# A convolution by butterfly matrices, attention and experts on one core: when input images are loaded in the first phase, and when GpSimd makes the butterfly matrices

## The chip, the cores and the metric

The kernel runs on one core of a Trainium2 chip. Its engines each work through their own queue in order: TensorE (PE, with its weight loads listed apart as PEld), VectorE (DVE), ScalarE (ACT), GpSimd (POOL) and SyncE (SP), which here issues the DMA transfers. The metric is the time on the device in microseconds (us); less is better.

## The reference, cut to what matters

The input is 32 images of 128 channels and 64 x 64 pixels, in 32-bit floats. Layer 0 normalises each image over groups of four channels, multiplies rows and columns by butterfly matrices (six levels of complex 2 x 2 twiddles each), mixes channels for every frequency with the weights, which have been transformed in the same manner, transforms back, keeps the real part and adds the input. Layer 1 is attention over channels and a mixture of eight experts of which two are used.

```python
def butterfly_lastdim(x, tw, increasing_stride):
    ...
        for idx in range(log_n):
            log_stride = idx if cur else log_n - 1 - idx
            stride = 1 << log_stride
            t = tw[blk, idx].reshape(n // (2 * stride), stride, 2, 2)
            xr = x.reshape(b, n // (2 * stride), 2, stride)
            x = jnp.einsum('djik,bdkj->bdij', t, xr).reshape(b, n)
...
x_f = tensor_product(xc, _c(k11), _c(k12), False)
w_f = tensor_product(wc, _c(kd1), _c(kd2), False) * math.sqrt(H * W)
prod = jnp.einsum('bihw,oihw->bohw', x_f, w_f)
out = tensor_product(prod, _c(k21), _c(k22), True)
return jnp.real(out)
...
x = x + _L0_conv_ref(_gn(x), L0_conv_weight, L0_conv_kd1, L0_conv_kd2, L0_conv_k11, L0_conv_k12, L0_conv_k21, L0_conv_k22)
t = _to_tokens(x)
t = t + _L1_attn_ref(_ln_t(t), L1_attn_Wk, L1_attn_bk, L1_attn_Wv, L1_attn_bv)
t = t + _L1_ffn_ref(_ln_t(t), L1_ffn_router_w, L1_ffn_router_b, L1_ffn_expert_w, L1_ffn_expert_b)
```

## The kernel before, in words

There are three phases. The first (lines 158 to 538) normalises each image and carries it into frequencies; the second (541 to 702) mixes the channels, frequency by frequency; the third transforms back and does layer 1. The change is in the first alone.

In the first phase an image goes through these steps. Eight loads of 256 KB, x(b, 0) to x(b, 7) (`load`, line 303), fill one of three image buffers. DVE takes statistics of 512 columns at a time (`stats`, line 310, "bn" in the plan); `group_norm` gathers them: an aggregate ("ag") on DVE, two tiny matmuls "g1" and "g2" with small DVE steps "gm" and "gr" behind each, a power on GpSimd ("gp", line 345, tile grstd), and four scalings "nm" of 1024 columns, from image 4 on by DVE (line 358). Then PE turns the image over in four groups ("pz", line 369), whose results ACT copies to z (line 379). The first transform runs along w in eight pieces ("pv", line 392; ACT copies each to v, line 403), the second along h in eight pieces ("pf", line 414). Each pf piece is copied to f, six of eight by DVE and pieces 3 and 7 by ACT ("fo", line 424), and SP stores it in two transfers of 256 KB ("fs", line 432). All the products of PE share four PSUM buffers, "ps"; a pf copy that is late holds one of them. There are four buffers f.

Images overlap: in slot s PE works on pz of image s, pv of image s - 1 and pf of image s - 2, in quarters: one pz, two pv, two pf. The order on PE is the order in which the program adds the operations.

The order on the other engines is the planner's (`Plan`, line 25). Every operation is added with an engine, an assumed duration, a due time in slots of 27.5, what it comes after, and what buffers it takes and frees. The planner plays this through: an engine that falls free takes, of the operations that are ready, the one with the earliest due time; it never breaks one off. The order so found is written out as the program. The durations and due times are nothing more than means of ordering; on the chip an instruction starts when the one before it in its queue is done and its own semaphores are there. So an "after" that isn't a true dependence of data only moves an instruction in its queue.

`norm(b)` (line 443) adds the loads of image b, due from slot b - 2 on, after the turning-over of image b - 3, whose buffer they take; the program calls it ahead of the PE work of slot b - 2. It then adds four statistics operations of two pieces each, due at slot b - 1. `butterfly(m, ...)` (line 435) builds one of the three transform matrices from its twiddles: m = 1 on DVE at the start, m = 0 (for the weights) and m = 2 (for the transform back) on GpSimd, with an opening step ("unit") and six levels (lines 207 to 222). `select` (line 241) also runs on GpSimd. m = 0 is due from slot 3.2 and m = 2 from slot 7. What comes of m = 2 is used by `output_matrices` ("wo", DVE) and lets the load "wm" of the weights start on SP.

Of the kernel before, what the change touches and what calls it, by code (L numbers as in the profile page):

```python
# [90 lines left out]
def kernel(  # L91
# [15 lines left out]
    nc = tc.nc  # L107
    B = x.shape[0]
# [11 lines left out]
    pf = dram.tile([n, n, P * n], F32, name="pf")  # L120
# [37 lines left out]
    with ExitStack() as ph1:  # L158
# [9 lines left out]
        made, xs, zs, vs, tile_of = {}, {}, {}, {}, {}  # L168
        on_pe = []

        def add(key, engine, us, at, run, after=(), take=(), free=(), late=0.0):
            after = [made[k] for k in after if k in made]
            if engine == "PE":
                after += on_pe[-1:]
            made[key] = plan.add(engine, us, SLOT * at, run, after, take, free, late)
            if engine == "PE":
                on_pe.append(made[key])
# [5 lines left out]
        def twiddles(m):  # L183
            def run():
                t = tile_of["tw", m] = bp.tile([P, 6, 2, 2, 2, n // 2], F32, tag="tw", name=f"tw{m}")
                for ax in range(2):
                    nc.sync.dma_start(
                        t[ax * n : (ax + 1) * n].rearrange("p a i j c d -> p (a i j c d)"),
                        tw[m, ax].rearrange("a i j c d -> (a i j c d)").partition_broadcast(n),
                    )  # L190
            return run

        def unit(m, eng):
            def run():
                cur = tile_of["bf", m] = bp.tile([P, 2, n], F32, tag="bf", bufs=2, name=f"bf{m}_in")
                eng.tensor_tensor(cur[:, 0, :], ident[:, 0:n], ident[:, n : 2 * n], ALU.add)
                if m == 1:

                    eng.tensor_copy(
                        cur[lo, 0, :].rearrange("p (k r) -> p r k", r=2), ident[lo, 0:n].rearrange("p (r k) -> p r k", r=2)  # L200
                    )
                eng.memset(cur[:, 1, :], 0.0)
            return run
# [99 lines left out]
        def load(b, k):  # L303
            def run():
                if k == 0:
                    xs[b] = xp.tile([P, NPIX], F32, tag="x", name=f"x{b}")
                nc.sync.dma_start(xs[b][:, k * 512 : (k + 1) * 512], xv[b][:, k * 512 : (k + 1) * 512])
            return run

        def stats(b, k):  # L310
            def run():
                if k == 0:
                    tile_of["bs", b] = st.tile([P, 8, 6], F32, name=f"gbs{b}", tag="gbs", bufs=2)
                for j in range(2 * k, 2 * k + 2):
                    nc.vector.bn_stats(tile_of["bs", b][:, j, :], xs[b][:, j * 512 : (j + 1) * 512])
            return run

        def group_norm(b):
# [116 lines left out]
        def butterfly(m, engine, eng, at, us):  # L435

            before = {1: [], 0: [("b1", 5), "wi", ("nm", 4, 3)], 2: [("b0", 5), "wd"]}[m]
            add(("tw", m), "SP", 0.9, -3.0 if m == 1 else at - 0.3, twiddles(m), before, (), (), 4.0)
            add((f"b{m}", -1), engine, 2 * us / 7, at, unit(m, eng), before)
            for idx in range(6):  # L440
                add((f"b{m}", idx), engine, us, at + 0.01 * idx, level(m, idx, eng), [("tw", m), (f"b{m}", idx - 1)])

        def norm(b):

            at = b - 1
            for k in range(8):
                add(
                    ("x", b, k), "SP", 0.45, b - 2 + 0.1 * k, load(b, k), [("pz", b - 3, g) for g in range(4)],
                    ("x",) if k == 0 else (), (), 4.0,
                )  # L450
            for k in range(4):
                add(("bn", b, k), "DVE", 1.4, at + 0.02 * k, stats(b, k), [("x", b, 2 * k), ("x", b, 2 * k + 1), ("nm", b - 2, 3)])

        def norm_on_pe(b, step):
            if not 0 <= b < B:
                return
            at = b - 0.9
            if step == 0:
                gn = tile_of["gn", b] = group_norm(b)
                add(("ag", b), "DVE", 0.4, at, gn[0], [("bn", b, k) for k in range(4)])  # L460
                add(("g1", b), "PE", 0.3, at, gn[1], [("ag", b)], ("ps",))
                add(("gm", b), "DVE", 0.7, at, gn[2], [("g1", b)])
            else:
                gn = tile_of.pop(("gn", b))
                add(("g2", b), "PE", 0.3, at, gn[3], [("gm", b)])
                add(("gr", b), "DVE", 0.25, at, gn[4], [("g2", b)], (), ("ps",))
                add(("gp", b), "POOL", 0.6 if b >= 4 else 1.6, at, gn[5], [("gr", b)])
                for k in range(4):
                    add(("nm", b, k), *(("DVE", 0.85) if b >= 4 else ("ACT", 1.05)), at + 0.01 * k, gn[6][k], [("gp", b)])

        def piece(kind, b, g, at):
            if not 0 <= b < B:
                return
            if kind == "pz":
                add(
                    ("pz", b, g), "PE", 1.0, at, turn_over(b, g), [("nm", b, k) for k in range(4)],
                    ("ps",), ("x",) if g == 3 else (),
                )
                for r in range(2):
                    add(  # L480
                        ("zo", b, g, r), "ACT", 1.2, at, turned(b, g, r),
                        [("pz", b, g)] + [("pv", b - 2, k) for k in range(8)] + ([("zo", b, 0, 0)] if g or r else []),
                        (), ("ps",) if r else (),
                    )
            elif kind == "pv":
                add(
                    ("pv", b, g), "PE", 1.12, at, along_w(b, g),
                    [("zo", b, k, r) for k in range(4) for r in range(2)] + ["wi"], ("ps",),
                )
                add(  # L490
                    ("vo", b, g), "ACT", 1.02, at, w_out(b, g),
                    [("pv", b, g)] + [("pf", b - 2, k) for k in range(8)] + ([("vo", b, 0)] if g else []), (), ("ps",),
                )
            else:
                add(("pf", b, g), "PE", 1.95, at, along_h(b, g), [("vo", b, k) for k in range(8)], ("ps",))
                on_act = g % 4 == 3
                add(("fo", b, g), "ACT" if on_act else "DVE", 1.02 if on_act else 1.22, at, h_out(b, g), [("pf", b, g)], ("f",), ("ps",))
                add(("fs", b, g), "SP", 0.9, at, store(b, g), [("fo", b, g)], (), ("f",), 5.0)
# [5 lines left out]
        norm_on_pe(0, 0)  # L504
        norm_on_pe(0, 1)
        for s in range(B + 2):
            if s + 2 < B:
                norm(s + 2)
            for g in range(4):
                at = s + 0.25 * g  # L510
                if g == min(s, 3) - 1:
                    norm_on_pe(s + 1, 0)
                piece("pz", s, g, at)
                for k in range(2):
                    piece("pv", s - 1, 2 * g + k, at + 0.04 + 0.04 * k)
                if g == min(s, 3) - 1:
                    norm_on_pe(s + 1, 1)
                for k in range(2):
                    piece("pf", s - 2, 2 * g + k, at + 0.12 + 0.07 * k)
            if s == 0:  # L520
                norm_on_pe(1, 0)
                norm_on_pe(1, 1)
            if s == 3:
                butterfly(0, "POOL", nc.gpsimd, 3.2, 4.5)
                add("sel", "POOL", 2.5, 3.5, select, [("nm", 4, 3)])
            if s == 6:
                add("wr", "PE", 0.6, 6.0, weight_rows, [("b0", 5), "sel"], ("ps",))
                add("wd", "DVE", 0.8, 6.0, weight_matrices, ["wr"], (), ("ps",))
                butterfly(2, "POOL", nc.gpsimd, 7.0, 4.5)
                add("wo", "DVE", 1.2, 9.0, output_matrices, [("b2", 5)])  # L530
                add("wm", "SP", 0.5, 10.0, weight_taps, [("b2", 5)], (), (), 4.0)
            if 12 <= s < 16:
                k = s - 12
                add(("wr", k), "POOL", 5.0, s - 0.5, onto_rows(k), ["wm", ("pf", s - 3, 4)], ("f",))
                add(("wt", k), "PE", 1.1, s, rows_turned(k), [("wr", k)], ("ps",))
                add(("we", k), "DVE", 1.25, s, rows_out(k), [("wt", k)], (), ("ps", "f"))
# [4 lines left out]
    with ExitStack() as ph2:  # L541
# [11 lines left out]
        made, tile_of = {}, {}  # L553
# [118 lines left out]
        for w in range(n):  # L672
# [9 lines left out]
            for half in range(2):  # L682
                for t in range(4):
                    at = w + 0.5 * half + 0.125 * t
# [632 lines left out]
```

## The time and the profile before

| | us |
|---|---|
| time, median of 3 runs (lowest to highest) | 6383.51 (6376.77 to 6393.35) |
| the profiled execution's own time | 6385.87 |
| span of that execution, first to last instruction | 6384.2 |
| busy over the span: PE / PEld / DVE / ACT / POOL | 6125.7 / 4796.3 / 4201.4 / 3757.4 / 4201.5 |

The first weight load of the second phase stands in the trace at 978.81 us, so the first phase is some 15% of the time. Its stretches, busy time of each engine with the number of instructions in brackets, then the granted share of TensorE's clock, the mean busy share of the 16 DMA engines and GB/s:

```profile
core 0: us, PE busy (x) PEld busy (x) DVE busy (x) ACT busy (x) POOL busy (x), PEclk, DMA share, GB/s
0.00:60.37 60.37, 26.32 (x588) 24.40 (x588) 35.33 (x122) 38.40 (x50) 4.95 (x19) 0.83 0.47 156
...
913.07:978.80 65.73, 64.60 (x1443) 62.71 (x1441) 22.05 (x18) 31.71 (x39) 1.08 (x1) 1.00 0.67 231
```

The first row is the filling of the pipeline, the second its draining. What lies between is in the prediction.

What SP waits for between 60 and 913 us (us in total, times, longest):

```profile
SPq L432 <- DVE f L424: 155.9, 71, 6.5
SPq L307 <- PE pz L369: 144.6, 26, 6.3
SPq L432 <- DVE gmv L324: 115.2, 27, 10.2
```

A line of a timeline reads: start, duration, engine, line, operation, tile written <- tiles read, shapes, how many alike were merged, and in square brackets how long the engine stood idle before it and what ended that. "issue" means that the profile shows nothing that the engine waited for.

### The profile page before, as it was taken

Reading aid. Unit: us, or ns where it says so; the run is one execution under the profiler, and the core shown is the slowest. Engines: PE = TensorE matmul, PEld = TensorE weight load, DVE = VectorE, ACT = ScalarE, POOL = GpSimd, SP = SyncE. Lnnn points to the kernel's source line nnn. Section 1 sums busy time; section 2 is a strip of 40 time slices with the busy share of each in tenths; the row PEclk is TensorE's granted clock in tenths of the full one; section 3 lists DMA queues with packets and bytes.
Section 4 is the critical chain, followed back from the end, with each engine's and each line's share of the span. In section 5 each row is a group of like instructions: output and inputs, shape, how many; then the busy total and the mean of one; then the engine's idle time right before and its main releaser. Section 6 shows DMA issues by size and latency. Waiting matters only on the chain. (4 is left out here: it accounts for less than half of the span.)

```text
span 6384.2 us, 218347 instructions
## 1 busy us (share of the span) xinstructions
PE 6125.7 (96%) x94922; PEld 4796.3 (75%) x94922; DVE 4201.4 (66%) x7626; ACT 3757.4 (59%) x7089; POOL 4201.5 (66%) x3780
## 2 busy tenths in 40 slices
PE   7999999999999999969999999999999999999987
PEld 7899998999999999966666666666666666666653
DVE  5555544555555555527787877778787878787776
ACT  6666663444444444446666667666666666666752
POOL 2110005666666666606888888888888888888889
PEclk9999999999999999989999999999999999999999
DMA  5666656666666666553121222222222212121100
GB/s 200 214 208 226 218 207 173 158 161 159 159 156 158 157 159 158 135 140 93 62 95 62 94 64 90 69 86 74 80 79 67 93 62 96 60 95 64 67 19 25
DMA packets 556966, 756.55 MB, mean 119 GB/s; under 512 B 58467, under 2 KB 321893, under 8 KB 551909
## 3 DMA queue, kind: packets, MB, share of 16 engines
q1 hardware_dynamic: 554096, 741.38, 38.8%
q8 instruction: 745, 12.21, 0.8%
q14 instruction: 217, 1.77, 0.1%
q10 hardware_dynamic: 1908, 1.19, 0.1%
HBM read 406.80 MB, written 335.54 MB: 116 GB/s over the span
## 5 line engine op out<-in xcount | busy, mean ns | idle before, releaser
L1189 PE MATMUL pe<-ew_sb,xT 128*128 128x512 f32 x4096 | 1983.0, 601 | 53.6 <-DVE tm L1200 53.3
L1200 DVE TENSOR_TENSOR tm<-pe,oh 128x512 f32<-128x512 f32 x2048 | 1354.3, 684 | 562.3 <-PE pe L1189 418.0
L1211 POOL TENSOR_TENSOR tm<-tm 128x512 f32<-128x512 f32 x1024 | 1306.8, 1291 | 314.5 <-DVE tm L1200 262.0
L1189 PEld LDWEIGHTS pe<-ew_sb,xT 128*128 128x128 f32 x4096 | 690.5, 191 | 525.0 <-issue 328.7
L623 PE MATMUL m<-f,s 128*64 128x64 f32 x32768 | 1069.9, 224 | 5.9 <-POOL s L574 4.5
L623 PEld LDWEIGHTS m<-f,s 128*64 128x64 f32 x32768 | 999.4, 138 | 67.6 <-POOL s L574 4.8
L574 POOL COPY s<-l 128x512 f32<-128x512 f32 x512 | 547.9, 1103 | 735.0 <-issue 656.2
L612 ACT COPY f<-g 128x1024 f32<-128x1024 f32 x512 | 518.5, 1013 | 672.2 <-PE g L601 645.0
L612 DVE COPY f<-g 128x1024 f32<-128x1024 f32 x512 | 627.1, 1225 | 348.9 <-PE g L601 340.9
L1214 POOL TENSOR_TENSOR tk<-tk,tm 128x256 f32<-128x256 f32 x1024 | 759.1, 741 | 80.3
L828 ACT COPY u<-pu 64x512 f32<-64x512 f32 x1024 | 593.4, 579 | 310.5 <-PE pu L818 299.6
L601 PE MATMUL g<-c,wst 9*128 9x128 f32 x16384 | 727.1, 287 | 25.6 <-ACT f L612 3.5
L1212 POOL TENSOR_TENSOR tm<-tm 128x512 f32<-128x512 f32 x512 | 652.5, 1274 | 40.1
L601 PEld LDWEIGHTS g<-c,wst 9*128 9x128 f32 x16384 | 580.5, 187 | 109.6 <-DVE f L612 69.2
L818 PEld LDWEIGHTS pu<-qw,r 128*128 128x128 f32 x4096 | 504.8, 197 | 169.5 <-ACT u L828 91.6
L633 DVE COPY o<-m 64x1024 f32<-64x1024 f32 x256 | 314.0, 1227 | 470.0 <-ACT o L633 395.8
L818 PE MATMUL pu<-qw,r 128*128 128x128 f32 x4096 | 523.7, 283 | 63.0 <-ACT u L828 52.8
L345 POOL TENSOR_TENSOR grstd<-gms,mhalf 128x1 f32<-128x1 f32 x32 | 17.7, 553 | 789.2 <-DVE gms L341 760.1
L414 PE MATMUL pf<-ph,v 128*128 128x128 f32 x4096 | 497.2, 280 | 20.5 <-issue 13.5
L576 POOL TENSOR_SCALAR s<-l 128x512 f32<-128x512 f32 x256 | 503.3, 1966 | 0.0
L414 PEld LDWEIGHTS pf<-ph,v 128*128 128x128 f32 x4096 | 471.8, 193 | 32.1 <-issue 15.0
L1227 ACT COPY so<-po 128x512 f32<-128x512 f32 x256 | 150.8, 589 | 572.5 <-issue 413.1
(165 smaller groups left out, 8624.6 us busy)
## 6 DMA issues: line engine op xcount, KB each, us to landing
xf<-f SPq DMA_DIRECT2D x512, 256.0 KB, 3.8
l<-xf SPq DMA_DIRECT2D x1024, 128.0 KB, 3.3
pf<-o SPq DMA_DIRECT2D x1024, 128.0 KB, 2.4
r<-pf SPq DMA_DIRECT2D x512, 256.0 KB, 4.6
x<-in_x_dram SPq DMA_DIRECT2D x256, 256.0 KB, 5.5
y<-in_x_dram SPq DMA_DIRECT2D x32, 2048.0 KB, 8.5
out_dram<-so SPq DMA_DIRECT2D x256, 256.0 KB, 2.0
tw<-in_tw_dram SPq DMA_DIRECT2D x6, 384.0 KB, 6.9
```

The costliest lines, as they stand in the source:

```text
L414: nc.tensor.matmul(pl[:, j * P : (j + 1) * P], vs[b][:, 8 * g + j, :], ph.rearrange("h r m -> h (r m)"), start=True, stop=True,)
L574: nc.gpsimd.tensor_copy(dst, src)
L601: nc.tensor.matmul(pg[g // 2][:, g % 2, m * P : (m + 1) * P], wst[rows, 16 * half + 4 * t + m, :], c[rows].rearrange("r h k -> r (h k)"), ...
L612: copy(f.rearrange("i m (g o) -> i m g o", g=2), tile_of["g", w, half, t][k].rearrange("i g (o m) -> i m g o", o=4))
L623: nc.tensor.matmul(ps[hh * n : (hh + 1) * n, q, :], s[:, h].rearrange("i k b -> i (k b)")[:, B * r : B * r + n], f[:, h, r, :], start=(r = ...
L818: nc.tensor.matmul(ps[:, k, :], rs[b, e][:, k * P : (k + 1) * P], qw.rearrange("w r m -> w (r m)"), start=True, stop=True,)
L828: nc.scalar.copy(u[r * n : (r + 1) * n, :, oh * n + 8 * e : oh * n + 8 * e + 8], ps[oh * n : (oh + 1) * n, :, r * n : (r + 1) * n].rearran ...
L1189: nc.tensor.matmul(ps, tile_of["xT", b, i // 4][:, i % 4, :], ew_sb[:, es, :].rearrange("d e c -> d (e c)"), start=True, stop=True,)
L1200: nc.vector.tensor_tensor(tile_of["tm", b, i // 2][:, i % 2, es, :], tile_of.pop(("pe", b, i, half)).rearrange("p (e c) -> p e c", c=P), t ...
L1211: nc.gpsimd.tensor_tensor(tm[:, k, 0:4, :], tm[:, k, 0:4, :], tm[:, k, 4:8, :], ALU.add)
L1212: nc.gpsimd.tensor_tensor(tm[:, :, 0:2, :], tm[:, :, 0:2, :], tm[:, :, 2:4, :], ALU.add)
L1214: nc.gpsimd.tensor_tensor(t[:, lo : lo + 2, :], t[:, lo : lo + 2, :], tm[:, :, m, :], ALU.add)
```

## The change

Three things are changed in the way the first phase is added to the plan.

Loads: from image 4 on, each load x(b, k) is added on its own behind the pf piece k of image b - 4 (`piece_of_image`), in the same slot b - 2 as before, and comes after that piece and after load k - 1. Images 0 to 3 keep their loads together.

Statistics: eight operations of one piece each in place of four of two, in the order of their pieces. `norm` for an image is added after the PE work of its slot in place of ahead of it, except for image 2.

GpSimd: the due times of the butterfly steps there, and of `select`, are put so late (99 slots on) that every other operation that is ready goes first. The loads of their twiddles keep their due times.

```diff
-                for j in range(2 * k, 2 * k + 2):
-                    nc.vector.bn_stats(tile_of["bs", b][:, j, :], xs[b][:, j * 512 : (j + 1) * 512])
+                nc.vector.bn_stats(tile_of["bs", b][:, k, :], xs[b][:, k * 512 : (k + 1) * 512])
...
             add(("tw", m), "SP", 0.9, -3.0 if m == 1 else at - 0.3, twiddles(m), before, (), (), 4.0)
+            at += 99 if engine == "POOL" else 0
             add((f"b{m}", -1), engine, 2 * us / 7, at, unit(m, eng), before)
...
+        def piece_of_image(b, k):
+
+            add(
+                ("x", b, k), "SP", 0.45, b - 2 + 0.1 * k, load(b, k),
+                [("pz", b - 3, g) for g in range(4)] + [("x", b, k - 1), ("pf", b - 4, k)],
+                ("x",) if k == 0 else (), (), 4.0,
+            )
+
         def norm(b):
 
             at = b - 1
+            for k in range(8) if b < 4 else ():
+                piece_of_image(b, k)
             for k in range(8):
-                add(
-                    ("x", b, k), "SP", 0.45, b - 2 + 0.1 * k, load(b, k), [("pz", b - 3, g) for g in range(4)],
-                    ("x",) if k == 0 else (), (), 4.0,
-                )
-            for k in range(4):
-                add(("bn", b, k), "DVE", 1.4, at + 0.02 * k, stats(b, k), [("x", b, 2 * k), ("x", b, 2 * k + 1), ("nm", b - 2, 3)])
+                add(("bn", b, k), "DVE", 0.7, at + 0.01 * k, stats(b, k), [("x", b, k), ("nm", b - 2, 3), ("bn", b, k - 1)])
...
-                add(("ag", b), "DVE", 0.4, at, gn[0], [("bn", b, k) for k in range(4)])
+                add(("ag", b), "DVE", 0.4, at, gn[0], [("bn", b, k) for k in range(8)])
...
         for s in range(B + 2):
-            if s + 2 < B:
-                norm(s + 2)
+            if s == 0:
+                norm(2)
             for g in range(4):
...
                 for k in range(2):
                     piece("pf", s - 2, 2 * g + k, at + 0.12 + 0.07 * k)
+                    if 4 <= s + 2 < B:
+                        piece_of_image(s + 2, 2 * g + k)
+            if 3 <= s + 2 < B:
+                norm(s + 2)
...
-                add("sel", "POOL", 2.5, 3.5, select, [("nm", 4, 3)])
+                add("sel", "POOL", 2.5, 99, select, [("nm", 4, 3)])
```

The order of the instructions on PE is the same in both programs. On GpSimd, the power step of image 8 stands behind the third of the six levels of m = 2 in place of the sixth, and that of image 5 one level of m = 0 earlier. On SP, in the middle of the phase, the loads of an image stand in this order among the stores: 0 and 1 behind the stores of piece 7 of the image before, 2 behind piece 1, 3 behind piece 2, 4 and 5 behind piece 3, 6 behind piece 5, 7 behind piece 6. On DVE the statistics of an image's pieces 6 and 7 and its aggregate stand ahead of the copy of pf piece 0, pieces 0 and 1 of the next image behind the copy of piece 1, and piece 2 between "gm" and "gr"; pieces 3 to 5 stand behind the copy of piece 5.

## The prediction

> **What bounds the kernel now.** The change touches only the first phase, so I read that stage alone, in four steps. First the busy times by stretch. I set the boundaries at starts of the first transpose group of an image (line 369): image 2 starts at 60.37 us, image 31 at 913.07; 540.95 to 570.12 is image 18, 885.74 to 913.07 image 30. Four short stretches are added. The columns are length, then busy time (instructions) of PE, PEld, DVE, ACT and POOL, then the granted clock, the DMA share, GB/s.
> ```profile
> 60.37:913.07 852.70, 812.54 (x19645) 775.40 (x19640) 469.69 (x666) 556.48 (x765) 82.33 (x230) 0.99 0.63 216
> 540.95:570.12 29.17, 27.85 (x679) 26.48 (x677) 16.20 (x24) 18.99 (x26) 0.55 (x1) 1.00 0.64 218
> 885.74:913.07 27.33, 27.22 (x678) 26.20 (x677) 10.84 (x14) 18.89 (x26) 0.55 (x1) 1.00 0.43 157
> 153.80:157.20 3.40, 3.40 (x18) 3.40 (x18) 1.88 (x2) 0.00 (x0) 0.00 (x0) 0.51 0.19 69
> 222.10:225.50 3.40, 3.40 (x19) 3.40 (x18) 1.34 (x4) 0.66 (x1) 3.19 (x10) 0.50 0.45 163
> 242.60:249.40 6.80, 4.82 (x118) 4.52 (x121) 6.63 (x14) 2.78 (x5) 0.57 (x2) 0.50 0.72 281
> 515.70:519.10 3.40, 3.40 (x16) 3.40 (x17) 2.63 (x5) 0.00 (x0) 0.00 (x0) 0.50 0.75 285
> ```
> PE sets the pace (812.54 of 852.70 us); DVE, ACT and DMA have room. Yet the 29 images take 852.70 / 29 = 29.40 us each, while image 30, during which no input image is loaded any more, takes 27.33 us with the same PE work and no gap. The pool to win from is (29.40 - 27.33) x 29 = 60 us, less some 5 us of extra PE work for the weights: 55 us.
>
> Second, what PE's weight loads wait for in that stretch (total, times, longest), and what DVE waits for:
> ```profile
> DVE gbs L315 <- DMA x<-in_x_dram: 99.3, 85, 14.7
> ...
> PEld pv L392 <- issue: 21.4, 94, 1.0
> ...
> PEld pf L414 <- issue: 15.0, 10, 2.5
> ...
> PEld pv L392 <- DVE f L424: 10.4, 15, 1.6
> ...
> PEld pz L369 <- issue: 6.0, 2, 5.6
> ...
> PEld pf L414 <- DVE f L424: 3.7, 11, 0.4
> ```
> Third, the timeline of image 18, which shows the wait for DVE being made:
> ```profile
> 545.34 2.92 DVE L315 BATCH_NORM_STATS2 gbs<-x 128x6 f32<-128x512 f32 x4 [2.36 <-DMA x<-in_x_dram]
> ...
> 549.33 0.69 DVE L315 BATCH_NORM_STATS2 gbs<-x 128x6 f32<-128x512 f32 x1 [1.07 <-DMA x<-in_x_dram]
> 549.94 1.21 DVE L424 COPY f<-pf 128x1024 f32<-128x1024 f32 x1
> ...
> 551.20 1.02 PEld L392 LDWEIGHTS pv<-pw,z 64*64 64x64 f32 x64 [1.16 <-DVE f L424]
> ```
> The statistics of image 20 stand on DVE ahead of the copy of pf. They wait for loads that SP issued in one burst, so the copy starts late, a PSUM buffer comes free late, and PE stops. Fourth, the timeline around image 8, where the wait called "issue" is really GpSimd:
> ```profile
> 228.61 0.16 DVE L341 TENSOR_SCALAR gms<-gps 128x1 f32<-128x1 f32 x1 [2.98 <-PE gps L338]
> ...
> 242.62 0.55 POOL L345 TENSOR_TENSOR grstd<-gms,mhalf 128x1 f32<-128x1 f32 x1
> ...
> 243.67 2.98 DVE L358 TENSOR_SCALAR x<-x,gms,grstd 128x1024 f32<-128x1024 f32 x4
> 244.55 1.57 PEld L369 LDWEIGHTS pz<-ident,x 128*128 128x128 f32 x8 [5.56 <-issue]
> ```
> The operand of grstd is there at 228.8, but grstd stands behind all six butterfly levels of the output twiddles, and PE idles 5.56 us for image 8.
>
> [...] the half-clock stretches above (0.50) are 3.4 us or twice that, and each lies at or behind one of PE's longest gaps (2.48 us before 153.64, 2.40 before 221.28, 5.56 before 244.55, 2.02 before 515.67). So a long gap costs more than itself. [...] The trace has that queue (q8, 745 packets, 12.21 MB), and I read the gaps inside PE groups that wait for nothing visible ("issue") as late refills: all those over 0.5 us, the 5.56 apart, lie 3 to 15 us into an image, which is where the loads and stores are densest. [...] From 538 to 551 us the DMA rows show nearly every slice at 9 tenths and 300 to 420 GB/s; from 561 to 565 they are idle.
>
> **The change part by part**, against the profiled execution's 6385.87 us (span 6384.2).
>
> 1. *GpSimd.* The operations are the same; the butterflies lose their due times, so grstd of image 8 comes after level three of six, and for image 5 one level earlier. A level takes 3.83 us (2.27 + 0.73 + 2 x 0.32 and hops). Level three ended at 231.2, so the normalisation (2.98 us) ends near 235, and image 8 would start at about 239: four us of slack. The gap of 5.56 us goes, and with it the half clock behind it: PE worked 4.82 us in 242.6 to 249.4 at 0.50, half of it lost, 2.4. Gain 8.0. Image 5 had no gap at its start, so nothing there. The last level ends some 0.5 us later; what waits for it (the copies into qw and hm on DVE, the load of the weights on SP) now stands ahead of a statistic and the copies of pf in image 8. I cost this at 0 to 2 us, and take 0.5: the pf copy can start 7.5 us into an image before PE stops.
>
> 2. *Loads.* 28 images have the same eight loads and sixteen stores as before. On SP the new order is: loads 0 and 1 behind the stores of the previous image, 2 behind piece 1, 3 behind 2, 4 and 5 behind 3, 6 behind 5, 7 behind 6. The wait of SP for the last transpose before load 0 (144.6 us over 26 images) goes, since that buffer is free well before; the stores of pieces 4 and 5 no longer stand behind it. Densest before: eight loads and eight stores of 256 KB, 4.2 MB, within some 9 us; after: four loads and eight stores, 3.1 MB, within 8 us, which the 400 GB/s seen above just carry.
>
> 3. *Statistics.* Eight of 0.69 us as before, but one by one; in the new order two (pieces 6 and 7) and the aggregate (0.36) stand ahead of the first pf copy of an image instead of all eight. I place it by an undisturbed image: quarters of 6.67 us, first pf group done at 5.2 us, second at 7.1, and its PSUM buffer must be copied out by about 8.9 (the start of the group that stopped in image 18 less its wait: 551.20 - 1.16 - 540.95 = 9.1). Load 7 goes out behind the store of piece 6, about 1.1 us into the image. With a landing time L the copy (1.23) ends at 1.1 + L + 0.69 + 0.36 + 1.23 + 0.1 = L + 3.5. The loads of before landed in 2.7/5.6/7.4 us (least, median, most), in bursts of eight, and in 3.2 us in a quieter stretch at 566; I take 4, so the copy ends at 7.5, and PE doesn't wait. Bounds: 0 at L up to 5.4, 2.0 us per image at L = 7.4. What DVE cost PE: 10.4 + 3.7 = 14.1 us in 26 waits, of which 0.17 each is the hop that any group has: 9.7. I take 9.0.
>
> 4. *Refills of instructions.* 15.0 + 21.4 us less 104 hops of 0.17, plus 0.3 of the pz row (6.0 - 5.56 less a hop): 19.0. Half clock behind three of them: 3 x 1.7 = 5.1. Together 24.1 us that depend on how dense the DMA is just then. The trace has no refill in a spread order: bounds 0 and 24; I take 0.7 of it, 17, because image 30, which has the stores but no loads, has no such gap.
>
> 5. *Start.* Statistics one by one let the two small DVE steps of image 1's normalisation pass ahead of one statistic each: 0.6 us, bound 0 to 1. The new waits (one more per statistic, odd late loads) I cost at 1.1.
>
> Sum: 8.0 - 0.5 + 9.0 + 17 + 0.6 - 1.1 = 33 us. The profiled execution becomes 6353; it stood 2.4 us over the median shown, so the forecast is 6350. The later phases have the same instructions and cancel.
>
> **Rivals.** *A: the refills stay late*, because sixteen stores still bunch between the last quarter and the next image's first. For it: the bunch only shrinks from 4.2 to 3.1 MB; against: image 30. Gain 8.0 - 0.5 + 9.0 + 0.6 - 1.1 = 16: 6367. *B: everything goes*, all 24.1 of part 4, all of part 3 and the rest of the pool: 55 us, 6328. *C, slower: the wait moves to load 7.* It is now the last thing that SP issues before the image whose first pf copy stands behind it. At L = 7.4 PE stops 2.0 us in each of 26 images, 52 us, the refills stay, and parts 1 and 3 (17) are the only gain: +35, 6418. It decides from the L at which the stop eats all gains, (17 / 26 = 0.65) L = 6.1 with the refills unrelieved, 6.7 with them relieved. Against it: a single load at the end of a thinner stream. *D: it does little*, because the written order is the planner's and the real order on each queue moves little: excluded for the loads, whose order in the program does change; for the rest 8 us at most, 6375.
>
> **How the numbers follow.** Forecast 0.60, A 0.15, B 0.10, C 0.09, D 0.06. About 0.3%, 19 us, is what can be told from no change. Faster by more: all of forecast and B, and two thirds of A: 0.80. Slower: C, 0.09. Same: the rest, 0.11. The range leaves out C and the deep end of B and takes in A and most of D: 6330 to 6372.
>
> **What would show it.** Right: images near 28 us between transposes; no 5.56 us wait ahead of image 8 and no half clock there; DVE waits for input loads far under 99 us; "issue" waits of pf under 7 us. Wrong: PE waiting for the DVE copy about 9 us into each image with the statistic of piece 7 ended by its load (C), or the issue gaps unchanged (A).

## The result, and the profile after

| | before | after |
|---|---|---|
| time, median of 3 runs each (lowest to highest), us | 6383.51 (6376.77 to 6393.35) | 6336.34 (6335.76 to 6336.63) |
| profiled execution / its span, us | 6385.87 / 6384.2 | 6336.34 / 6334.6 |
| first weight load of the second phase, us | 978.81 | 931.26 |
| first phase: fill / images 2 to 30 / drain, us | 60.37 / 852.70 / 65.74 | 57.73 / 807.26 / 66.27 |
| per image of the 29, us | 29.40 | 27.84 |

The ratio of the times is 0.9924, with a 95% interval from 0.9902 to 0.9947: 0.8% less, clear of the noise. Of the 49.5 us between the two profiled executions 47.55 lie ahead of the second phase, and 45.4 of those in the 29 images of the middle, as the table shows. Only the middle can be put down to the change. The fill is 57.73 us in after and 59.57 in a second profile of the same kernel (e10 below), so 2.6 us of it are within what varies by itself; and what follows the first phase took between 5397.4 and 5418.5 us in the twelve profiles of this document, with no change to it, so the 2.0 us there are too.

The busy times of after by stretch. The columns are those of the prediction's first view; 480.28 to 507.61 is one image.

```profile
core 0: us, PE busy (x) PEld busy (x) DVE busy (x) ACT busy (x) POOL busy (x), PEclk, DMA share, GB/s
0.00:57.73 57.73, 23.95 (x588) 22.19 (x589) 35.51 (x122) 37.61 (x49) 4.95 (x19) 0.88 0.48 164
57.73:864.99 807.26, 798.01 (x19646) 765.86 (x19640) 468.85 (x666) 556.37 (x766) 85.46 (x230) 1.00 0.69 228
...
480.28:507.61 27.33, 27.22 (x679) 26.20 (x677) 16.12 (x23) 18.89 (x26) 0.55 (x1) 1.00 0.70 234
```

PE has the same instructions, and in images 2 to 30 its clock is whole (1.00 in the second row). The last row is an image whose eight loads are running, with DMA at 0.70, and it takes the 27.33 us that before only image 30 took, the one without loads. Eleven of the 29 images now take 27.33. So loads as such need cost PE nothing.

What PE's weight loads and the statistics wait for in after, from 55 to 900 us (total, times, longest):

```profile
DVE gbs L314 <- DMA x<-in_x_dram: 115.4, 60, 3.5
...
PEld pv L391 <- issue: 17.1, 96, 0.6
...
PEld pf L413 <- ACT z L378: 7.1, 32, 0.6
...
PEld pv L391 <- DVE f L423: 1.8, 2, 1.6
...
PEld pf L413 <- issue: 1.2, 3, 0.6
```

The rows of pf at "issue" (15.0 before), of pv behind the copy (10.4) and of pz (6.0, no row now) are nearly gone. What stays in the pv row at "issue" is mostly the hop, the pause of 0.17 us that a pv group has behind a pz group even when nothing holds it up (as at 515.35 below). But the first row has grown, from 99.3 to 115.4: DVE waits for loads longer than before, and PE doesn't notice. The timeline of an image shows why:

```profile
507.61 0.91 PEld L368 LDWEIGHTS pz<-ident,x 128*128 128x128 f32 x8
...
508.41 0.46 SPq L307 DMA_DIRECT2D x<-in_x_dram  x1
...
511.91 0.69 DVE L314 BATCH_NORM_STATS2 gbs<-x 128x6 f32<-128x512 f32 x1 [2.16 <-DMA x<-in_x_dram]
512.64 0.37 DVE L323 BATCH_NORM_AGGREGATE gmv<-gbs 128x2 f32<-128x48 f32 x1
512.92 1.16 DVE L423 COPY f<-pf 128x1024 f32<-128x1024 f32 x1
...
515.35 1.96 PEld L391 LDWEIGHTS pv<-pw,z 64*64 64x64 f32 x128 [0.17 <-issue]
```

The image starts at 507.61. Load 7 is issued at 508.41, its statistic starts at 511.91, so the load took 3.5 us; the copy of pf ends at 514.08, 6.5 us into the image. The group of PE that needs the buffer starts at 515.35 after nothing but the hop. The wait of 2.16 us on DVE lies in slack. In images 4 to 29 of after this copy ends 6.4 us into the image (median), at 7.5 at the latest but for image 8, where it ends at 10.3.

All gaps of over 0.3 us ahead of a weight load in images 2 to 30, less the hop of 0.17, summed by what ended them, with the time in those images at half clock (the stretches of 0.50; PE's work in them counts half as lost, since weight loads of pf follow each other there every 213 ns and at full clock every 112, medians of before):

| | before | after |
|---|---|---|
| "issue": refills of instructions | 19.1 in 21 | 1.6 in 5 |
| DVE's copies of pf | 9.7 in 23 | 2.0 in 2 |
| grstd of image 8 | 5.4 | none |
| ACT's copies (z, f) and others | 1.9 in 4 | 2.2 in 5 |
| all gaps | 36.0 | 5.9 |
| lost to half clock | 7.5 | 0 |

Gaps and clock make 37.6 of the 45.4 us. The other 7.8 don't lie elsewhere; the table takes too much off. A hop is to be taken from a gap only where the same weight load has one in after too, and most of these loads have none (21 of the 23 behind DVE's copies, for example, start in the middle of a group or behind one without a hop). It can be counted without hops: PE has the same 94,922 weight loads in both programs, so the time from each load to the next can be set against that of the same two loads in the other trace. The difference, before less after, summed over images 2 to 30 by what ended the gap in the trace that has it:

| us | gaps of before | gaps of after | together |
|---|---|---|---|
| "issue": refills of instructions | 22.64 | -1.40 | 21.24 |
| DVE's copies of pf | 13.47 | -2.55 | 10.92 |
| grstd of image 8 | 5.64 | none | 5.64 |
| ACT's copies and others | 1.45 | -1.61 | -0.16 |
| other loads at half clock (1.91 behind grstd, 4.82 behind refills) | 6.73 | none | 6.73 |
| all other loads, some 19,400 | | | 1.07 |
| sum | | | 45.44 |

Last, GpSimd's part, the timeline of after where image 8 is normalised:

```profile
221.09 0.55 POOL L344 TENSOR_TENSOR grstd<-gms,mhalf 128x1 f32<-128x1 f32 x1
...
221.68 2.99 DVE L357 TENSOR_SCALAR x<-x,gms,grstd 128x1024 f32<-128x1024 f32 x4 [2.27 <-POOL grstd L344]
...
235.38 0.19 DVE L238 COPY hm<-bf 64x64 f32<-64x64 f32 x1
...
235.79 0.69 DVE L314 BATCH_NORM_STATS2 gbs<-x 128x6 f32<-128x512 f32 x1
...
236.81 2.29 DVE L423 COPY f<-pf 128x1024 f32<-128x1024 f32 x2
238.02 1.02 PEld L391 LDWEIGHTS pv<-pw,z 64*64 64x64 f32 x64 [1.62 <-DVE f L423]
```

grstd is there at 221.6 in place of 243.2, and the wait of 5.56 us is gone. Two smaller ones come in its place: the scalings, 2.27 us late, hold up a copy of pf in that slot, which costs PE 0.75 us at 225.85 (and z's copy 0.56), and 13 us later the copies into qw and hm stand with a statistic ahead of a copy of pf, for 1.62 us.

### The profile page after: what moved, and what is told of

Its sections match the earlier page's. It is cut to its first block, busy times and chain, and to the rows that moved or that the text cites. A ratio compares the mean times of both kernels' runs of the same rounds, so it can differ in the third digit from the quotient of the medians.

```text
span 6334.6 us, 218332 instructions
## 1 busy us (share of the span) xinstructions
PE 6111.2 (96%) x94922; PEld 4788.4 (76%) x94922; DVE 4195.7 (66%) x7626; ACT 3756.7 (59%) x7089; POOL 4206.0 (66%) x3780
## 5 line engine op out<-in xcount | busy, mean ns | idle before, releaser
L882 DVE BATCH_NORM_STATS2 bs<-tk 128x6 f32<-128x128 f32 x2048 | 447.9, 279 | 55.8 <-ACT tk L913 43.7
```

## The experiments

Three accounts were set against each other: the gain is that of GpSimd; it is that of DVE, which no longer waits ahead of a copy; or it is that of the DMA, where transfers spread out let PE's instructions arrive in time. Each time below is a median (runs in brackets), the ratio is to runs of the kernel before on the same chip, with its 95% interval. The other columns are from one profiled execution each: start of the second phase, length of images 2 to 30, and in these the gaps at "issue" (GpSimd's apart), the gaps behind DVE's copies, both less a hop each as in the first table of gaps, and the stretches at half clock. The length of images 2 to 30 is the better measure, since the start of the second phase has the fill in it, which varies from 57.3 to 60.4 us.

| | time, us | ratio | phase 2 at | images 2 to 30 | "issue" | DVE | half clock |
|---|---|---|---|---|---|---|---|
| before | 6383.51 (3) | | 978.81 | 852.70 | 19.1 | 9.7 | 17.0 |
| after | 6336.34 (3) | 0.9924 [0.9902, 0.9947] | 931.26 | 807.26 | 1.6 | 2.0 | 0 |
| e1 GpSimd alone | 6378.37 (12) | 0.9995 [0.9986, 1.0003] | 973.42 | 849.45 | 21.5 | 8.2 | 13.6 |
| e2 loads alone | 6342.58 (4) | 0.9942 [0.9925, 0.9959] | 938.21 | 812.19 | 2.9 | 0 | 6.8 |
| e3 burst, statistics late | 6376.12 (12) | 0.9984 [0.9976, 0.9993] | 974.65 | 849.23 | 30.5 | 0.4 | 17.0 |
| e4 four more loads, early | 6373.35 (20) | 0.9982 [0.9975, 0.9988] | 974.43 | 842.91 | 25.5 | 3.0 | 17.0 |
| e5 four more loads, ahead of load 7 | 6443.6 (1) | | 1028.88 | 898.49 | 4.8 | 53.3 | 68.0 |
| e6 statistics in pairs | 6355.84 (4) | 0.9941 [0.9926, 0.9956] | 944.11 | 818.98 | 1.2 | 1.2 | 0 |
| e7 output matrices later | 6347.98 (4) | 0.9927 [0.9911, 0.9943] | 931.97 | 807.02 | 3.0 | 0 | 0 |
| e8 burst in mid-image | 6362.96 (4) | 0.9946 [0.9925, 0.9966] | 954.13 | 829.79 | 19.2 | 2.1 | 0 |
| e9 a load behind each store | 6345.73 (5) | 0.9938 [0.9925, 0.9952] | 929.93 | 806.77 | 3.4 | 0 | 0 |
| e10 the change again | 6338.25 (5) | 0.9927 [0.9914, 0.9939] | 932.18 | 805.79 | 1.9 | 1.3 | 0 |

e5 to e8 ran where the kernel before took 6393.81 us (7 runs), e9 and e10 where it took 6384.38 (9), e1 to e4 where it took 6385.25 (39). Compare ratios across these groups, not times. The ratios are the recorded ones and need not be the quotient of the two medians: for e1 that would be 0.9989. e5 is a single execution, of which only the profile is used. The executions profiled in e3 and e8 were the slowest of theirs, 7.3 and 8.6 us above the median, so the gaps shown for these two are rather too large than typical.

**The parts by themselves.** e1 is before with the late due times of GpSimd; e2 is after without them.

```diff
 e1, on before
+            at += 99 if engine == "POOL" else 0
-                add("sel", "POOL", 2.5, 3.5, select, [("nm", 4, 3)])
+                add("sel", "POOL", 2.5, 99, select, [("nm", 4, 3)])
 e2, on after: these two undone
```

> The kernel before with only the late due times on GpSimd; loads and statistics as before. If the parts add up as in the forecast, the 5.56 us gap ahead of image 8 and the half clock behind it go and nothing else: the second phase's first weight load (978.8 us before, 931.3 with the whole change) at about 971, time about 6376. If the GpSimd part carries more than its 8 us (for instance because later gaps follow from it), below 965 and 6370.

> The whole change without the late due times on GpSimd. The gap ahead of image 8 returns and is longer than before, since PE now arrives some 10 us earlier at the same six butterfly levels: about 9 us and some 2.4 us of half clock, less the waits of 1.6 and 1.3 us in images 7 and 8 that the changed kernel has there: second phase from about 940, time about 6345. If the parts simply add: 8 us, 6344 and 939. The two can be told apart by the gap itself (5.6 or 9 us).

GpSimd alone brings the second phase 5.4 us forward, but 3.0 of that is the fill; images 2 to 30 take 3.3 us less, since the refill gaps (21.5 against 19.1) and the half clock apart from that behind grstd (13.6 against 10.2) are larger there. By the recorded ratio its time can't be told from before (1.0003 is in the interval), though the medians lie 6.9 us apart. The loads and statistics alone bring most of the gain, 40.5 us in images 2 to 30. Together that is 43.8, close to the 45.4 of the whole change, so these two parts add up. e2 keeps the wait that GpSimd's part removes, and so shows its price in the new order:

```profile
PEld pz L368 <- issue: 6.4, 1, 6.4
```

That is 6.4 us, between the 5.6 and the 9 that had been expected, and a stretch of 6.8 us at half clock behind it, as it was before.

**DVE relieved, the burst kept.** e3 keeps the loads in one burst at the start of a slot, but moves the statistics, one by one, behind copies of pf, so that no copy waits for a load. The order of loads and stores on SP is that of e1 (two loads, the stores of a piece, one load, the stores of a piece, five loads); the orders on PE, ACT and GpSimd are also those of e1; so e3 differs from e1 on DVE alone.

```diff
-                [("pz", b - 3, g) for g in range(4)] + [("x", b, k - 1), ("pf", b - 4, k)],
+                [("pz", b - 3, g) for g in range(4)],
...
-                add(("bn", b, k), "DVE", 0.7, at + 0.01 * k, stats(b, k), [("x", b, k), ("nm", b - 2, 3), ("bn", b, k - 1)])
+                add(("bn", b, k), "DVE", 0.7, at + 0.01 * k, stats(b, k), [("x", b, k), ("nm", b - 2, 3), ("bn", b, k - 1), ("fo", b - 4, (1, 1, 2, 2, 5, 5, 6, 6)[k])])
...
+            if 4 <= s + 2 < B:
+                for k in range(8):
+                    piece_of_image(s + 2, k)
             for g in range(4):
```

> The whole change, but the eight loads of an image stand on SP in one burst as in the kernel before, and the statistics are put behind the copies of pf pieces 1, 2, 5 and 6 of the slot, so that DVE never waits for loads ahead of a copy. If the gaps called issue are instruction refills held up by the dense transfers, they stay (pf and pv rows of PE's weight loads together 36 us, about 19 beyond the usual hops, with half clock behind the longest): second phase from 955 to 965, time 6360 to 6370. If those gaps came from DVE's lateness, they go with it: second phase below 938, time at most 6343.

```profile
PEld pv L391 <- issue: 29.6, 99, 2.0
PEld pf L413 <- issue: 19.6, 13, 2.9
...
PEld pv L391 <- DVE f L423: 0.7, 2, 0.6
```

The waits for DVE are gone (0.7 us), as they should be, and the time has hardly moved: images 2 to 30 take 849.23 us against 849.45 in e1, and the medians of twelve executions each are 2.2 us apart. Neither expectation is met; the second phase starts later than in both. The gaps at "issue" have grown, from 19.1 in before and 21.5 in e1 to 30.5 us. So DVE's 9.7 us and the refills' 19.1 were no sum: with one removed, the other grew by as much. Why is less clear. One reading, which is an estimate, is that a PE that stands still for DVE gives its refill time to arrive, and that without this wait the refill is late instead; but of the growth from e1 to e3 only 3.7 us lie at the refills ahead of which e1 had waited for DVE (11.1 us there), 6.0 at others, and the execution profiled in e3 was its slowest. One such gap, in the timeline of e3 and in its busy times by stretch:

```profile
211.55 13.21 SPq L431 DMA_DIRECT2D xf<-f  x8
...
214.66 1.64 PEld L413 LDWEIGHTS pf<-ph,v 128*128 128x128 f32 x14
219.04 3.61 PEld L413 LDWEIGHTS pf<-ph,v 128*128 128x128 f32 x18 [2.74 <-issue]
```

```profile
206.00:213.00 7.00, 7.00 (x192) 6.77 (x195) 2.42 (x3) 5.56 (x11) 1.20 (x4) 1.00 0.97 339
213.00:218.90 5.90, 3.49 (x134) 3.23 (x126) 1.29 (x3) 3.99 (x6) 1.08 (x4) 1.00 0.91 286
218.90:222.30 3.40, 3.25 (x15) 3.26 (x16) 2.42 (x3) 0.00 (x0) 3.17 (x11) 0.50 0.15 52
```

Of 32 weight loads of one pf group 14 run; then PE stands 2.74 us in the middle of the group, with nothing in the program to wait for; then 18 run at half clock (0.50 in the third row). DMA had been busy at 0.97 and 0.91. The records of single transfers name the cause more closely: on q8, the queue that the profile lists as "instruction" (745 packets of 16 KB in before and in after), a transfer began at 216.66, when PE already stood, and ended 1.44 us ahead of the restart. All 26 gaps of this kind in e3 from image 2 on that are over 0.5 us restart 1.21 to 1.60 us after the end of such a transfer, and so do 16 of 16 in before and 4 of 4 in after. The gap of GpSimd doesn't (7.6 us in before, 9.0 in e2), so the two kinds called "issue" can be told apart.

The place of the gaps fits this. All twelve programs here have the same 94,922 weight loads on PE, so the loads can be counted. Of the 110 gaps over 0.5 us at "issue" in the twelve traces between 57 and 905 us (GpSimd's apart) 108 lie within 1.2 loads of places 127.22 loads apart, the same in every run; by chance some 2% would. One transfer on q8 comes for every 127 weight loads too (19,472 loads and 153 transfers in after between 60 and 860 us). So the gaps recur at the spacing of the transfers on q8. The 127.22 was fitted to these gaps. That PE stands there because its next instructions have not come is what I infer from this and from the restarts; no view shows it as such.

**More traffic at the two places.** e4 and e5 add four loads of 256 KB per image into tiles that nothing reads; nothing is left out. In e4 they stand behind load 1, among the stores; in e5 ahead of load 7.

```diff
+                nc.sync.dma_start(spare[j], xv[b][:, j * 512 : (j + 1) * 512])
...
 e4, behind the add of load 1
+                    add(("more", b, j), "SP", 0.01, b - 2 + 0.1, more(b, j), [("x", b, 1), ("more", b, j - 1)])
 e5, ahead of the add of load 7, which comes after them
+                    add(("more", b, j), "SP", 0.01, b - 2 + 0.69, more(b, j), [("x", b, 6), ("pf", b - 4, 7), ("more", b, j - 1)])
```

> The whole change plus four more loads of 256 KB per image (rows of the input into spare buffers that nobody reads), issued on SP behind load 1 of an image, where no statistic or copy that DVE waits for stands behind them before the store of piece 0. If dense transfers hold up the refills, issue waits of PE come back to between 5 and 20 us beyond the hops: time 6342 to 6360. If density doesn't matter: 6336 within 3.

> The same four additional loads as in the run that put them behind load 1, but issued ahead of load 7, so that it goes out 1.8 us later and lands about 3 us later; the order on DVE is that of the changed kernel, statistic 7 and the aggregate ahead of the first pf copy. By the forecast's deadline (the copy has to end by 8.9 us into an image; it ended at 6.5 in the changed kernel's image 18) it would now end between 9 and 10: waits of PE's pv weight loads for the DVE copy between 3 and 25 us in total, against 1.8 in the changed kernel and 3.7 with the loads behind load 1. If DVE's lateness isn't what holds PE, these stay under 4 us. The refill gaps come as with the loads behind load 1 in both cases: second phase from 970 to 990.

e4, what PE's weight loads wait for:

```profile
PEld pv L391 <- issue: 33.2, 100, 3.3
PEld pf L413 <- issue: 11.2, 11, 2.1
...
PEld pv L391 <- DVE f L423: 3.7, 4, 1.5
```

The waits are at "issue", as the refills' account has it, not at DVE; their size I had put too low (13 us and more over the time expected). e4 also moves 1 MB per image more in all, so by itself it doesn't separate the place from the amount. e5 has the same amount:

```profile
DVE gbs L314 <- DMA x<-in_x_dram: 238.8, 69, 8.9
PEld pv L391 <- DVE f L423: 58.1, 28, 3.2
...
PEld pf L413 <- issue: 4.0, 5, 2.1
```

Here the wait is DVE's, 2 us in nearly every image and half clock behind most (68.0 us), and the refills are almost on time (4.8 us) with the same traffic, which had not been expected. This fits the estimate above that a PE that waits for DVE gives its refills time. It is the prediction's rival C made real. One image of e5, which started at 584.19, in its timeline:

```profile
586.81 0.43 SPq L307 DMA_DIRECT2D x<-in_x_dram  x1
...
592.75 0.69 DVE L314 BATCH_NORM_STATS2 gbs<-x 128x6 f32<-128x512 f32 x1 [6.62 <-DMA x<-in_x_dram]
...
593.76 2.28 DVE L423 COPY f<-pf 128x1024 f32<-128x1024 f32 x2
594.98 1.80 PEld L391 LDWEIGHTS pv<-pw,z 64*64 64x64 f32 x64 [2.02 <-DVE f L423]
```

Load 7 was issued at 586.81 and its statistic starts at 592.75; the first of the two copies ends about 10.8 us into the image, and PE, which would have gone on at 8.8 (594.98 - 2.02 - 584.19), waits 2.02. The deadline of 8.9 us that the prediction reckoned with holds; in the image of after shown above the copy beats it by 2.4 us. I had expected 3 to 25 us of such waits and a start of the second phase from 970 to 990, and got 53 and 1028.88.

**The same burst, in mid-image.** e8 adds all eight loads behind pf piece 3, in mid-image, with their statistics behind the copy of piece 5. On SP they stand as five loads, the stores of one piece and three loads.

```diff
-                [("pz", b - 3, g) for g in range(4)] + [("x", b, k - 1), ("pf", b - 4, k)],
+                [("pz", b - 3, g) for g in range(4)] + [("x", b, k - 1), ("pf", b - 4, 3)],
...
-                    if 4 <= s + 2 < B:
-                        piece_of_image(s + 2, 2 * g + k)
+                    if 4 <= s + 2 < B and 2 * g + k == 3:
+                        for j in range(8):
+                            piece_of_image(s + 2, j)
```

> The eight loads of an image together again, but behind pf piece 3 in the middle of a slot, away from the stores of pieces 4 to 7 and of the next image's first pieces; statistics behind the copy of piece 5. If it is the sum of loads and stores in one stretch that holds up the refills, a burst in a gap between stores does little harm: 6336 to 6350, second phase from 931 to 945. If any burst of eight loads holds them up: 6365 to 6378 as with the burst at its old place.

```profile
PEld pv L391 <- issue: 28.6, 99, 2.6
PEld pf L413 <- issue: 8.9, 9, 2.0
```

Images 2 to 30 take 829.79 us, in the middle between before and after, and neither expectation is met. The amount of traffic is that of after. A burst of eight in mid-image still makes 19.2 us of refill gaps, against 30.5 at the start of an image (e3); no half clock follows in these images. So the place of a burst counts, and even at the better place a burst costs more than loads one by one, which stand among the stores in after and e9 and leave 1.6 and 3.4 us.

**Statistics one by one.** e6 is after with the statistics in four pairs, as before.

```diff
-            for k in range(8):
-                add(("bn", b, k), "DVE", 0.7, at + 0.01 * k, stats(b, k), [("x", b, k), ("nm", b - 2, 3), ("bn", b, k - 1)])
+            for k in range(4):
+                add(("bn", b, k), "DVE", 1.4, at + 0.02 * k, stats(b, k), [("x", b, 2 * k), ("x", b, 2 * k + 1), ("nm", b - 2, 3)])
```

> The whole change, but statistics again as four operations of two pieces each, placed by the planner: the pair 2, 3 now falls between gr and the scalings, the pair 6, 7 ahead of the first copy as before. If what counts is that loads are spread, within 5 of 6336. If statistics one by one are a needed part of it, the pair holds up the scalings and the copies of pieces 4 and 5 by some 0.6 us, 0.3 to 0.4 beyond what PE's buffers allow, in each of 26 images: 6344 to 6350.

The timeline of one image of e6:

```profile
529.19 1.27 DVE L315 BATCH_NORM_STATS2 gbs<-x 128x6 f32<-128x512 f32 x2
...
530.39 2.96 DVE L358 TENSOR_SCALAR x<-x,gms,grstd 128x1024 f32<-128x1024 f32 x4
533.26 2.35 DVE L424 COPY f<-pf 128x1024 f32<-128x1024 f32 x2
...
536.34 3.65 PEld L414 LDWEIGHTS pf<-ph,v 128*128 128x128 f32 x32 [0.56 <-ACT z L379]
```

A pair (1.27 us) now stands ahead of the scalings where a single one (0.69) stood; the copies behind them shift, and PE waits 0.56 us at its last pf group. The gaps behind ACT's copy of z grow from 1.6 us in 4 to 10.9 in 28, and images 2 to 30 take 11.7 us more. Statistics one by one are a part of the gain.

**What is left.** e7 moves the copies into qw and hm behind the copy of pf piece 2 of image 6. e9 adds to e7 that each load comes after its own store, statistics 6 and 7 after the copy of piece 1 of the next image, and statistic 2 after the scalings. e10 is the change unaltered.

```diff
 e7
-                add("wo", "DVE", 1.2, 9.0, output_matrices, [("b2", 5)])
...
+            if s == 9:
+                add("wo", "DVE", 1.2, 9.0, output_matrices, [("b2", 5), ("fo", 6, 2)])
 e9, besides
-                [("pz", b - 3, g) for g in range(4)] + [("x", b, k - 1), ("pf", b - 4, k)],
+                [("pz", b - 3, g) for g in range(4)] + [("x", b, k - 1), ("pf", b - 4, k), ("fo", b - 4, k)],
```

> The whole change, but the five copies that use the finished output matrix stand on DVE behind the copy of pf piece 2 in image 8 instead of ahead of pieces 0 and 1. If these copies, waiting for the last butterfly level, make the 1.62 us wait of PE in image 8, it goes: second phase from 929.6, time about 6334.5. If it was a load that was late, no difference: 6336.

> The whole change with three more steps: each load goes behind the store of its own piece (one load for each piece, none in pairs), statistics 6 and 7 stand behind the next slot's copies 0 and 1 so that no copy waits for them, statistic 2 behind the scalings; the copies of the output matrix later as in the run for them. If density of transfers at an image's start makes the refill gaps that are left (2.2 us) and statistics 6 and 7 hold nothing up, 2 to 8 us are left to win of the changed kernel's 27.84 us per image (27.33 at least, about 27.5 with the weights' extra work): second phase from 923 to 930, time 2 to 8 below the changed kernel in the same job. If the bunch of stores alone sets what is left: within 2 of it.

> The changed kernel itself, for comparison on the same chip: second phase from 929 to 934, a ratio to the kernel before of 0.9924 within its interval.

In e7 the wait of 1.62 us is gone, so the copies into qw and hm did make it, but nothing is won: images 2 to 30 take 807.02 us (807.26 and 805.79 in the two profiles of the change). The gaps at "issue" are 1.4 us larger, none of them in images 7 to 9 and no more than the scatter of such small sums. In e9 the statistics scarcely wait:

```profile
DVE gbs L314 <- DMA x<-in_x_dram: 9.3, 7, 2.7
```

That is 9.3 us in place of 115.4, and nothing comes of it: images 2 to 30 take 806.77 us against e10's 805.79, and the median is 7.5 us above e10's, where 2 to 8 below had been expected. DVE's waits for loads were worth nothing any more. No version here beats the change.

## Why the prediction was right, and which terms were off

It said 6350 us with a range from 6330 to 6372; 6336.34 was measured. The mechanism of the likeliest case is the one that the runs show, and rival C did not happen: the copy of pf ended 6.4 us into an image (median), where 7.5 was reckoned. Most misses of size went one way, and the range, 42 us wide, took them in. By its parts, measured on the same two loads as in the second table of gaps:

- *GpSimd, 8.0 less 0.5.* The wait and its half clock are gone, 5.64 + 1.91, nearly as sized. What stands late in its place was put at 0.5, with 2 as the bound, and measured 2.55, the two waits behind DVE's copies. This term was too favourable.
- *Loads and refills, 17 of 24.1.* This term was mis-sized most: 21.24 us of gaps and 4.82 of half clock went, 26.1. "0.7 of it" was a choice between bounds, on the ground that the sixteen stores still bunch. The stores do, and the refills are in time all the same. Rival A (refills stay) is refuted, and e3 and e8 show that bunched loads bring the gaps back.
- *DVE's copies, 9.0.* 13.47 us went. The prediction took a hop of 0.17 us off each of 26 waits as one "that any group has"; most of these loads have no hop when nothing holds them up. The same deduction made part 4's pool too small. What the sum got wrong in kind is that it added this part to the refills as if they were independent: e3, with DVE's waits gone and the burst kept, needs as long for images 2 to 30 as e1. In the change both went at once. Loads spread with the waits for DVE left in place were not tried.
- *Start, 0.6.* The fill shrank by 2.6 us, but it is 57.37 us in e1, with statistics in pairs, and 59.57 in e10, with statistics one by one. So the effect that was claimed isn't shown.
- *New waits, 1.1.* DVE's waits for loads grew by 16 us, but PE shows nothing of them: the gaps behind ACT and others rose by 0.16 us.

The sum of 33 against 49.5 measured is thus 9.1 from the refills, 4.5 from DVE's copies, 0.9 of new waits that didn't come and 1.1 spread over all other loads, less 2.5 at GpSimd's part; that makes 46. The other 3.5 lie in fill, drain and the later phases, which vary by that much without a change. The outcome lay between the forecast and rival B (everything goes, 6328), nearer to B.

One reading of the prediction was wrong: the rate from 538 to 551 us was not 300 to 420 GB/s throughout. The slices of the view go from 158 to 466 while it is busy, though nearly all show 9 tenths.

Of the signs that the prediction named, images near 28 us (27.84), no 5.56 us wait, no half clock and pf's issue waits under 7 us (1.2) came. One was wrong: DVE's waits for loads far under 99 us. They rose to 115.4. Spreading the loads did not make DVE wait less; it made it wait where no copy was late for it.

That the gaps at "issue" are late refills was an estimate when the prediction was made. The restarts 1.21 to 1.60 us behind the end of a transfer on q8 (16 of 16 in before) bear it out. PE has the same instructions in after and in e3, with 1.6 us of such gaps in 29 images and 30.5, so here they depend on the traffic beside them.

On the clock, the four stretches at half clock in images 2 to 30 of before are three of 3.41 us and one of 6.83. In the 3.41 us straight ahead of them PE was busy (by the profile, with modelled ends) for 1.01, 1.21, 0.00 and 1.60 us, in order of time. The length of the gap alone doesn't tell: the gap of 2.02 us in before, which lies in the first row below, had half clock behind it, and the longest gap of e8, 2.63 us, which is split between the third row and the fourth, had none:

```profile
512.25:515.66 3.41, 1.60 (x65) 1.34 (x54) 1.53 (x3) 3.19 (x5) 0.00 (x0) 1.00 1.00 324
515.66:519.07 3.41, 3.39 (x16) 3.40 (x17) 2.64 (x5) 0.00 (x0) 0.00 (x0) 0.50 0.75 288
```

```profile
709.78:713.19 3.41, 1.82 (x111) 1.68 (x110) 3.41 (x6) 3.27 (x5) 0.00 (x0) 1.00 1.04 397
713.19:716.61 3.42, 2.52 (x36) 2.45 (x37) 0.36 (x1) 1.07 (x2) 0.00 (x0) 1.00 0.51 191
```

The first two rows are before, the others e8; the columns are those of the busy times above. PE is busy for 1.60 of 3.41 us (47%) in the first and 1.82 (53%) in the third, and the clock (third number from the end) is 0.50 only behind the first. What decides between the two was not shown.

## What to carry to other kernels

Where PE stops inside a group with nothing to wait for, look at the DMA just then: here instructions came by DMA too (q8, 745 transfers of 16 KB), and with loads that nobody needed yet in a burst beside the stores PE stood 30.5 us in 29 images (e3), with the loads spread 1.6 (after). So spread such loads, one behind each piece of PE's work. Don't add up waits of one engine without a test (here DVE's copies and the refills): removing one alone can let the other grow. Judge a wait by the deadline of what is queued behind it, here 8.9 us into an image, not by its length: 115 us of DVE's waiting cost PE nothing in after, 239 us cost it 53 in e5. And where two programs give an engine the same instructions, compare their starts one by one; it found 7.8 us that gaps and hops had missed.

## What was not expected of the hardware

The transfers on q8 weren't slower where PE stood for them longer. Their median was 0.96 us in before, after, e3, e4 and e8 alike (144 to 153 transfers each between 60 and 860 us); what differs is when they start, and PE goes on 1.2 to 1.6 us after the end of one. What holds back the start, other transfers ahead of it or the request itself, no run here separates.

Loads one by one didn't land much sooner than in bursts: 3.0/4.5/6.6 us (least, median, most) in after, 2.7/5.6/7.4 in before.

The time became steadier: the three runs of after lie within 0.9 us, the five of e10 within 7.2, the three of before within 16.6 and the 39 beside e1 to e4 within 24.3. With the late refills gone there is less that depends on chance; that they are the cause of the scatter is an inference, not shown.
